# Layer 1 of a two-layer network: up values by seven block products, and layernorms on ScalarE

## The chip, the cores and the metric

The kernel runs on one core of a Trainium2 chip. The metric is the device time of one execution in microseconds (us). TensorE does matrix products into PSUM, VectorE, ScalarE and GpSimd work on elements, and SyncE issues transfers. The page of the profile calls them PE, DVE, ACT, POOL and SP; PEld is TensorE's loading of weights.

## The reference, cut to what matters

Two layers work on x of shape (4, 512, 256). Each normalises the rows and adds an attention branch and a feed-forward branch. Layer 0 (an mLSTM with its own MLP, and a low-rank mixture of experts) is the same in both kernels. Layer 1 is the place of the change:

```python
def _layernorm(x, axis=-1, eps=1e-05):
    m = jnp.mean(x, axis=axis, keepdims=True)
    v = jnp.var(x, axis=axis, keepdims=True)
    return (x - m) / jnp.sqrt(v + eps)
...
def _L1_ffn_ref(x, w_gate, w_up, w_down):
    h = jax.nn.silu(jnp.einsum('bsh,hi->bsi', x, w_gate)) * jnp.einsum('bsh,hi->bsi', x, w_up)
    h_sparse = _sparsify_2to4(h)      # of each four neighbours the two largest by |h| stay
    return jnp.einsum('bsi,ih->bsh', h_sparse, w_down)
...
xn = _layernorm(x, axis=-1)
x = x + _L1_attn_ref(xn, L1_attn_weight_qkv, L1_attn_weight_out) + _L1_ffn_ref(xn, L1_ffn_w_gate, L1_ffn_w_up, L1_ffn_w_down)
```

`w_gate` and `w_up` are 256 x 1024, `w_down` is 1024 x 256, all in float32. The attention of layer 1 is among the 4 entries of the first axis, 16 heads of 16, causal.

## The kernel before

The 512 rows are cut into NJ = 4 blocks j of 128 rows. A block holds its rows of all four batch entries, so a transposed block `xT` (tile `xnT`) is two tiles (k = 0, 1) of 128 features by S = 512 columns.

**Order.** Nothing is ordered by hand. Generators (`flow`) yield the time at which they can go on, and the class `Clock` keeps a model of each engine's time (`took`, `issue`), by which the generators are interleaved while the program is written. Each engine then executes its instructions strictly in that order. All instructions pass through one helper, so the profile gives line 222 for nearly all of them, and work is told apart by tile names.

**A block of layer 1.**
- `front_rows(j)` makes the layernorm (`layernorm`: bn_stats, bn_aggr, a power of -1/2 on GpSimd, a scaling, on VectorE) into tile `xn`, and eight transposes `pt` with two ScalarE copies into `xnT`. `following_rows(j + 1)` runs it beside block j and then `other_sides`, four subtractions of quarters of `xnT` into tile `xd`. Block 0's layernorm runs at the end of layer 0.
- `rows(j)` takes the 1024 columns of the feed-forward in two halves, f0 = 0 and 4. A half is 512 columns, or four chunks of 128, in the tile `hs`.
- The gate values of a half come from seven block products in place of eight (`Sevens.pairs`). The weights' sides (`sides`: four GpSimd operations for each pair of chunks) are made once, ahead, in rooms of tiles that layer 0 has left. Each product is two matmuls of 128x128 by 128x256. They go into the PSUM tiles `x`, `y` and the standing bank `z`, in a chain: products x and y, ScalarE copies of x to z and of y to a room (`copied`), further products added in the same banks, a ScalarE copy of x, and VectorE additions (`added`) of PSUM to the copies. The rooms lie in the tiles `w_up` and `w_down` of layer 0. The chain's second part, `last`, runs as a generator of its own.
- `gate` applies ScalarE's Silu into `hs`.
- The up values of a half are four chunks `up` of 128x512 from `project` (two matmuls each, weights in tile `lora`), each multiplied into `hs` by VectorE.
- `sparsified` makes ScalarE's absolute values `hm`, comparisons `c`, `rest`, `t`, `keep`, and two multiplications on VectorE.
- `attention_rows` makes q, k and v (`qk_ps`, `v_ps`, copied by ScalarE); `attend_rows` the attention, with products `pd` on GpSimd and their sums `sc`, `o` on VectorE, then transposes `pt<-ident,o`.
- `finish_rows` sums the output `yp` of a block over 10 terms, adds it to x and writes it out. It runs late, beside the next blocks.

A matmul of the program is two instructions in the profile. Tiles reused from layer 0 keep that layer's name: `w_gate` is here the down weights, `wguT` the gate weights, `WdT` the qkv weights.

Of the kernel before, what the change touches and what calls it, by code (L numbers as in the profile page):

```python
# [9 lines left out]
AF = mybir.ActivationFunctionType  # L10
ALU = mybir.AluOpType
AX = mybir.AxisListType

P = 128
B, S, D = 4, 512, 256
NJ = S // P
KD = D // P
H, DQK, DV = 8, 16, 32
FF, NF = 1024, 1024 // P
# [15 lines left out]
def layers_kernel(ctx: ExitStack, tc: tile.TileContext, io: dict, out: bass.AP):  # L35
# [17 lines left out]
    class Clock:  # L53
# [100 lines left out]
        def issue(self, kind, op, args, kw, us=None, what=None):  # L154
            operands = [*args, *kw.values()]
            aps = [o for o in operands if hasattr(o, "tensor") and hasattr(o, "offset")]
            out, ins = aps[0], aps[1:]
            if "out" in kw:
                out = kw["out"]
                ins = [i for i in aps if i is not out]  # L160

            shared = [i for i in ins if str(i.space) == "PSUM"]
            start = max(self.free[kind], self.ready(out, *shared, reads=True, but=kind),
                        self.ready(*ins, but=kind))
            if kind == "pe" and start > self.free["pe"]:
                self.stalls.append((self.free["pe"], start - self.free["pe"], out.tensor.name))
            if kind == "act":
                f = next((o for o in operands if isinstance(o, AF)), None)
                if f is not None and f not in self.ANY:
                    table = f in self.SILU  # L170
                    if table != self.table:
                        start += 1.28
                    self.table = table
            if us is None:
                us = self.took(kind, op, out, ins, operands, start)
            end = self.free[kind] = start + us
            end += 0.2 if kind == "pe" else 0.08
            for ap, w, r in [(out, end, 0.0), *((i, 0.0, end) for i in ins)]:
                lo, hi = self.part(ap)
                name = ap.tensor.name  # L180
                spans = self.known(name)
                if w and lo == 0 and len(spans) > 64:
                    spans[:] = [s for s in spans if s[2] > start - 50 or s[3] > start - 50]
                spans.append((lo, hi, w, r, kind))
# [12 lines left out]
    def new(pool, shape, tag, bufs=None, dtype=F32):  # L197
        count[0] += 1
        kw = {} if bufs is None else {"bufs": bufs}
        t = pool.tile(shape, dtype, tag=tag, name=f"{tag}_{count[0]}", **kw)  # L200
        clock.ring(t, (id(pool), tag), bufs or (2 if tag in ("xn", "xnT") else 1))
        return t
# [244 lines left out]
    def inv_sqrt(o, i):  # L447
        n = i.shape[1]
        pool.tensor_tensor(out=o, in0=i, in1=mhalf[:, 0:n], op=ALU.pow)

    def layernorm(pool, x, xn, ms=None):


        stats = new(pool, [P, B, 6], "stats", 2)
        mv = new(pool, [P, B, 2], "mv", 2)
        rstd = new(pool, [P, B], "rstd", 2)
        for b in range(B):
            dve.bn_stats(stats[:, b, :], x[:, b, :])
            dve.bn_aggr(mv[:, b, :], stats[:, b, :])
            yield flow.spare()  # L460
        var = mv[:, :, 1]
        dve.tensor_scalar(rstd, var, 1e-5, None, ALU.add)
        if ms is not None:
            dve.reciprocal(ms, rstd)
        inv_sqrt(rstd, rstd)
        if ms is not None:

            dve.tensor_tensor(ms, ms, var, ALU.mult)
            dve.tensor_scalar(ms, ms, 1e-6, None, ALU.add)
        yield from flow.wait(rstd)  # L470
        for b in range(B):
            dve.tensor_scalar(
                xn[:, b, :], x[:, b, :], mv[:, b, 0:1], rstd[:, b : b + 1], ALU.subtract, ALU.mult
            )
# [26 lines left out]
    def sides(w, rooms, by):  # L501

        v = w.rearrange("p k (q m c) -> p k q m c", m=2, c=P)
        for i in range(len(rooms) // 3):
            q = slice(2 * i, 2 * i + 2)
            a11, a12, a21, a22 = v[:, 0, q, 0, :], v[:, 1, q, 0, :], v[:, 0, q, 1, :], v[:, 1, q, 1, :]
            s1, s2, s4 = rooms[3 * i : 3 * i + 3]
            for o, a, b, op in ((s1, a21, a22, ALU.add), (s2, s1, a11, ALU.subtract),  # L510
                                (a21, a11, a21, ALU.subtract), (s4, a12, s2, ALU.subtract)):
                by.tensor_tensor(out=o, in0=a, in1=b, op=op)

        def kept(n):
            return lambda q: rooms[q // 2 * 3 + n][:, q % 2, :]

        return {"a11": lambda q: v[:, 0, q, 0, :], "a12": lambda q: v[:, 1, q, 0, :],
                "a22": lambda q: v[:, 1, q, 1, :], "s3": lambda q: v[:, 0, q, 1, :],
                "s1": kept(0), "s2": kept(1), "s4": kept(2)}
# [93 lines left out]
    both = ctx.enter_context(tc.tile_pool(name="both", bufs=2))  # L613
    xTs = {}

    def front_rows(j):

        xn = new(both, [P, B, D], "xn")
        yield from layernorm(both, x_sb[j], xn)
        xT = new(both, [P, KD, S], "xnT")  # L620
        for k in range(KD):
            yield from flow.wait(xn, banks=1)
            transposed(lambda l, k: xn[:, l, k * P : (k + 1) * P], xT, k)
        yield from flow.wait(xT)
        xTs[j] = xT
# [891 lines left out]
    f_down = weight("f_down", D, "w_gate")  # L1517
    aoT = weight("aoT", D, "w_out")
    rooms = [t[:, KD * FF + i * 2 * P : KD * FF + (i + 1) * 2 * P] for i in range(3)]
    for name, n in (("wvg", KD * V), ("w_og", KD * D)):  # L1520
        t = new(wts, [P, n], name)
        rooms += [t[:, i : i + 2 * P] for i in range(0, n - 2 * P + 1, 2 * P)]
    rooms = [t.rearrange("p (q c) -> p q c", c=P) for t in rooms]
    gate_sides = sides(f_gate, rooms[0:6], pool)
    t = [new(wts, [P, NF * D], name) for name in ("w_up", "w_down")]
    copies = [t[i % 2][:, i // 2 * S : (i // 2 + 1) * S] for i in range(8)]

    def room():
        copies.append(copies.pop(0))
# [4 lines left out]
    with ExitStack() as l1:  # L1534
# [165 lines left out]
        def room_of_sides():  # L1700
            return new(wk1, [P, 4, HALF], "xd", 2)

        def following_rows(j):
            yield from front_rows(j)
            bs[j] = other_sides(xTs[j], room_of_sides(), dve)

        def rows(j):
            if j + 1 < NJ:
                flow.add(following_rows(j + 1), 3, turn=-2)
            b = bs[j]  # L1710
            while j >= 2 and j - 2 not in out_of:
                yield flow.soon(0.2)
            for f0 in range(0, NF, 4):
                hs = new(wk1, [P, 4, S], "hs", 4)
                gated.setdefault(j, []).append(hs)
                there, done = set(), set()

                def part(m, half, hs=hs):
                    return hs.rearrange("p (i m) n -> p i m n", m=2)[
                        :, :, m, half * HALF : (half + 1) * HALF]  # L1720

                def gate(m, half, t, free, part=part, there=there):
                    act.activation(part(m, half), t.rearrange("p (i n) -> p i n", i=2), AF.Silu)
                    there.add((m, half))
                    free()

                def then(hs=hs, done=done, n=2 * j + f0 // 4):
                    while len(done) < 4 or sum(map(len, halves.values())) < n:
                        yield flow.soon()
                    yield from sparsified(j, hs)  # L1730

                first, last = sevens.pairs(gate_sides, b, f0 // 2, gate)
                yield from first
                flow.add(last, turn=-2)
                for n in range(4):
                    yield from flow.wait(banks=1)
                    up = mm_ps("up")
                    project(up, f_up, xTs[j], (f0 + n) * P, P)
                    clock.held.add(up.tensor.name)

                    def rest(n=n, up=up, hs=hs, there=there, done=done):
                        while (n % 2, 0) not in there or (n % 2, 1) not in there:
                            yield flow.soon(0.2)
                        yield from flow.wait(up, hs[:, n, :])
                        clock.held.discard(up.tensor.name)
                        dve.tensor_tensor(hs[:, n, :], up, hs[:, n, :], ALU.mult)
                        done.add(n)

                    flow.add(rest(), turn=-2)
                flow.add(then(), turn=-1)  # L1750
            flow.add(finish_rows(j), turn=1)
# [52 lines left out]
```

## Time and profile before

| | |
|---|---|
| median of 3 runs | 759.52 us (759.51 to 759.94) |
| the profiled execution | 760.13 us, its span 758.4 us |
| busy in the span: PE, PEld | 751.7 and 539.0 us |
| DVE, ACT, POOL | 490.0, 234.9 and 163.4 us |
| DMA | 25.44 MB, mean 34 GB/s |

The times of the runs are of whole executions. The profile is of one execution of its own: its span goes from the first to the last instruction, and 1.73 us lie around it. The busy times overlap; how they lie in the two layers is told with the prediction.

### The profile page before, as it was taken

To read this page: it belongs to the slowest core of one execution; us is meant where nothing else is said; L and a number is where in the kernel's file an instruction comes from. 1 tells how busy PE (TensorE), PEld (TensorE's weight loads), DVE (VectorE), ACT (ScalarE), POOL (GpSimd) and SP (SyncE) were. 2 spreads that over 40 slices of the span, in tenths; PEclk is the share of its full clock that TensorE was granted. 3 is DMA by queue.
4 is the path that set the end of the run, shared out by engine and by line. 5 is a ranking of instruction groups with operands and counts; after the bars stand their busy time and mean duration, and the time that the engine had idled before them with its cause. 6 is when DMAs were issued, how large, how long until landed. Compare 5 with 4: busy or idle time off the path is not lost.

```text
span 758.4 us, 9984 instructions
## 1 busy us (share of the span) xinstructions
PE 751.7 (99%) x3890; PEld 539.0 (71%) x3890; DVE 490.0 (65%) x1099; ACT 234.9 (31%) x479; POOL 163.4 (22%) x154
## 2 busy tenths in 40 slices
PE   9999999999999999999999999999999999999998
PEld 6786878766578776766778775756766668668587
DVE  5777586766644887654377745433678989788571
ACT  3334133432222333131323122120253642542310
POOL 6230052150132050113020023210322333112000
PEclk9999999999999999999999999999999999999999
DMA  7930000030000020000030310001000000000001
GB/s 232 301 112 1 2 0 1 6 108 0 2 1 1 30 83 1 1 1 1 1 111 1 111 44 14 1 0 56 0 1 0 1 1 25 4 0 29 0 15 42
DMA packets 18959, 25.44 MB, mean 34 GB/s; under 512 B 2784, under 2 KB 12768, under 8 KB 18912
## 3 DMA queue, kind: packets, MB, share of 16 engines
q1 hardware_dynamic: 17824, 24.53, 10.2%
q8 instruction: 30, 0.49, 0.3%
q10 hardware_dynamic: 1088, 0.28, 0.2%
q14 instruction: 17, 0.14, 0.1%
HBM read 22.65 MB, written 2.16 MB: 33 GB/s over the span
## 4 chain that ended last, share of the span: by engine, by line
PE 91%; DVE 7%; ACT 1%; issue 0%; POOL 0%; DVEq 0%; POOLq 0%
PE chunk L222 18%; PE yp L222 16%; PE up L222 15%; PE acc L222 11%; PE gp L222 7%; PE x L222 3%; PE qk_ps L222 3%; PE pt L222 2%; PE vp L222 2%; PE o_ps L222 2%; PE lp L222 2%; PE v_ps L222 2%; PE y L222 2%; PE qk L222 1%; PE sums L222 1%; PE hv L222 1%
## 5 line engine op out<-in xcount | busy, mean ns | idle before, releaser
L222 ACT ACTIVATE sl<-chunk 128x256 f32<-128x256 f32 x132 | 50.6, 384 | 122.2 <-PE chunk L222 106.6
L222 PE MATMUL chunk<-low,lora 128*128 128x256 f32 (+1 forms) x384 | 85.8, 383 | 1.6 <-DVE he_pair L222 1.1
L222 PE MATMUL chunk<-xnT,wguT 128*128 128x256 f32 (+1 forms) x384 | 83.2, 383 | 0.0
L222 PEld LDWEIGHTS chunk<-xnT,wguT 128*128 128x128 f32 (+1 forms) x384 | 64.2, 181 | 20.4 <-issue 8.8
L222 PEld LDWEIGHTS chunk<-low,lora 128*128 128x128 f32 (+1 forms) x384 | 63.7, 181 | 17.1 <-issue 5.1
L222 DVE SCALAR_TENSOR_TENSOR sl<-sl,chunk 128x256 f32<-128x256 f32 x132 | 54.7, 414 | 30.0 <-ACT sl L222 29.4
L222 PE MATMUL gp<-featT,w_gate 128*128 128x512 f32 x128 | 60.3, 593 | 0.0
L222 PE MATMUL up<-featT,w_up 128*128 128x512 f32 x128 | 60.3, 593 | 0.0
L222 PE MATMUL up<-xnT,lora 128*128 128x512 f32 x128 | 58.4, 592 | 0.0
L222 PE MATMUL yp<-w_down,hid 128*128 128x256 f32 x256 | 56.6, 379 | 0.0
L222 PE MATMUL yp<-w_gate,hs 128*128 128x256 f32 x256 | 56.1, 379 | 0.0
L222 PEld LDWEIGHTS yp<-w_down,hid 128*128 128x128 f32 x256 | 48.4, 190 | 8.2 <-issue 1.9
L222 PEld LDWEIGHTS yp<-w_gate,hs 128*128 128x128 f32 x256 | 48.6, 190 | 6.6
L222 DVE SCALAR_TENSOR_TENSOR tmp<-tmp,gp 128x512 f32<-128x512 f32 x32 | 22.0, 687 | 43.1 <-ACT tmp L222 43.1
L222 ACT ACTIVATE tmp<-gp 128x512 f32<-128x512 f32 x32 | 19.1, 598 | 91.3 <-PE gp L222 91.3
L222 POOL TENSOR_TENSOR ss<-ss,mhalf 128x32 f32<-128x32 f32 x4 | 22.0, 5503 | 101.2 <-DVE ss L222 101.2
L222 PEld LDWEIGHTS up<-featT,w_up 128*128 128x128 f32 x128 | 24.1, 190 | 27.6 <-issue 26.5
L222 PEld LDWEIGHTS gp<-featT,w_gate 128*128 128x128 f32 x128 | 24.0, 190 | 27.5 <-issue 26.8
L222 PE MATMUL acc<-WdT,hid 128*128 128x256 f32 (+1 forms) x192 | 41.1, 382 | 0.0
L222 PE MATMUL acc<-tmp,lora 128*128 128x512 f32 x80 | 40.4, 595 | 0.0
L222 PEld LDWEIGHTS up<-xnT,lora 128*128 128x128 f32 x128 | 24.3, 190 | 22.5 <-issue 21.0
L222 POOL TENSOR_TENSOR pd<-k,q 128x512 f32<-128x512 f32 (+2 forms) x12 | 23.3, 1944 | 70.7 <-ACT k L222 44.1
(252 smaller groups left out, 1263.8 us busy)
## 6 DMA issues: line engine op xcount, KB each, us to landing
ct<-m_dram SPq DMA_DIRECT2D x8, 1024.0 KB, 8.1
x<-in_x SPq DMA_DIRECT2D x3, 512.0 KB, 9.7
out<-x SPq DMA_DIRECT2D x6, 256.0 KB, 2.1
w_gate<-in_w_gate SPq DMA_DIRECT2D x1, 1024.0 KB, 6.7
w_up<-in_w_up SPq DMA_DIRECT2D x1, 1024.0 KB, 7.7
w_down<-in_w_down SPq DMA_DIRECT2D x1, 1024.0 KB, 10.2
wguT<-in_f_gate SPq DMA_DIRECT2D x1, 1024.0 KB, 4.8
lora<-in_f_up SPq DMA_DIRECT2D x1, 1024.0 KB, 4.9
```

Of the source, the lines that this page charges most:

```text
L222: return tc.keep_in_program_order(f(*args, **kw))
```

## The change

Three things change in layer 1.
- The up values of each block's second half (f0 = 4) come from `sevens.pairs` with the up weights' sides. The four `project` chunks of that half go. `up_too` multiplies each of the four quarters of a half by the gate in `hs`, as soon as the gate's quarter is there.
- The up weights' sides are made by four more GpSimd operations ahead, in rooms 6 to 8, which take in the tiles `wq` and `wk` of layer 0. One of the eight rooms for copies becomes a place for squares that nobody reads, so seven are left.
- The layernorms of blocks 1 to 3 are made by `norm_by_scalar`: four ScalarE sums (`accum_out`), four shifts, four squares with sums, four scalings, with two small VectorE operations and GpSimd's power between. The generator starts at once, not 3 us later.

The writer's model also learns that an instruction with `accum_out` writes two things.

```diff
+            extra = kw.get("accum_out")
...
+            ins = [i for i in ins if i is not extra]
...
-            for ap, w, r in [(out, end, 0.0), *((i, 0.0, end) for i in ins)]:
+            written = [out] if extra is None else [out, extra]
+            for ap, w, r in [*((o, end, 0.0) for o in written), *((i, 0.0, end) for i in ins)]:
...
-    def front_rows(j):
+    def front_rows(j, norm=None):
...
-        yield from layernorm(both, x_sb[j], xn)
+        yield from norm(x_sb[j], xn) if norm else layernorm(both, x_sb[j], xn)
...
-    for name, n in (("wvg", KD * V), ("w_og", KD * D)):
+    for name, n in (("wvg", KD * V), ("w_og", KD * D), ("wq", KD * P), ("wk", KD * P)):
...
-    gate_sides = sides(f_gate, rooms[0:6], pool)
+    gate_sides, up_sides = (sides(w, room, pool) for w, room in (
+        (f_gate, rooms[0:6]), (f_up[:, :, FF // 2 :], rooms[6:9])))
...
+    unread_squares = copies.pop()[:, 0:D]
...
+        def norm_by_scalar(x, xn):
+
+            sums = new(sm, [P, 3, B], "sums", 2)
+            mean, ss, rstd = (sums[:, n, :] for n in range(3))
+            for b in range(B):
+                act.activation(xn[:, b, :], x[:, b, :], AF.Identity, accum_out=mean[:, b : b + 1])
+                yield flow.soon(0.5)
+            yield from flow.wait(mean)
+            dve.tensor_scalar(mean, mean, -1.0 / D, None, ALU.mult)
+            yield from flow.wait(mean)
+            for b in range(B):
+                act.activation(xn[:, b, :], x[:, b, :], AF.Identity, bias=mean[:, b : b + 1])
+                yield flow.soon(0.5)
+                act.activation(
+                    unread_squares, xn[:, b, :], AF.Square, accum_out=ss[:, b : b + 1])
+                yield flow.soon(0.5)
+            yield from flow.wait(ss)
+            dve.tensor_scalar(ss, ss, 1.0 / D, 1e-5, ALU.mult, ALU.add)
+            inv_sqrt(rstd, ss)
+            yield from flow.wait(rstd)
+            for b in range(B):
+                act.mul(xn[:, b, :], xn[:, b, :], rstd[:, b : b + 1])
+                yield flow.soon(0.5)
...
-            yield from front_rows(j)
+            yield from front_rows(j, norm_by_scalar)
...
-                flow.add(following_rows(j + 1), 3, turn=-2)
+                flow.add(following_rows(j + 1), 0, turn=-2)
...
-                for n in range(4):
+
+                def up_too(m, half, t, free, part=part, there=there, done=done):
+                    def rest():
+                        h = part(m, half)
+                        while (m, half) not in there:
+                            yield flow.soon(0.2)
+                        yield from flow.wait(h, t)
+                        dve.tensor_tensor(
+                            h, t.rearrange("p (i n) -> p i n", i=2), h, ALU.mult)
+                        done.add((m, half))
+                        free()
+
+                    flow.add(rest(), turn=-2)
+
+                if f0:
+                    first, last = sevens.pairs(up_sides, b, 0, up_too)
+                    yield from first
+                    flow.add(last, turn=-2)
+                for n in range(0 if f0 else 4):
```

## The prediction

> **What bounds the kernel now.** I read the page first, then the busy time by stage, TensorE's timeline in the second layer, the groups of instructions by shape, and the timelines of VectorE and GpSimd where they meet.
>
> ```profile
> PE 751.7 (99%) x3890; PEld 539.0 (71%) x3890; DVE 490.0 (65%) x1099; ACT 234.9 (31%) x479; POOL 163.4 (22%) x154
> ...
> PEclk9999999999999999999999999999999999999999
> ...
> PE 91%; DVE 7%; ACT 1%; issue 0%; POOL 0%; DVEq 0%; POOLq 0%
> ```
>
> TensorE is busy all the time at the full granted clock, and 91% of the chain of waits is its own work. The stage that the change touches begins with the matmul that opens layer 1's PSUM bank z, at 536.87 us. The stage view gives (columns: time, then busy time and instructions of PE, PEld, DVE, ACT, POOL):
>
> ```profile
> 0.00:536.87 536.87, 533.43 (x3032) 381.51 (x3033) 322.66 (x845) 153.97 (x334) 116.63 (x123) 1.00 0.14 43
> 536.87:758.40 221.53, 218.28 (x859) 157.45 (x857) 167.38 (x254) 80.90 (x145) 46.77 (x31) 1.00 0.03 10
> ```
>
> In layer 1 TensorE works 218.28 of 221.53 us, and the rest is almost all the end, after its last matmul. VectorE has 167.38, ScalarE 80.90. So what counts is how much matmul time goes, and how much of it comes back as waits of TensorE, which takes its instructions strictly in the order written. TensorE's timeline shows the prices (start, length, instructions):
>
> ```profile
> 642.52 1.03 PE L222 MATMUL z<-xnT,wguT 128*128 128x256 f32 x4
> 643.38 1.03 PE L222 MATMUL y<-xnT,wguT 128*128 128x256 f32 x4
> 644.25 1.37 PE L222 MATMUL pt<-ident,o 128*128 128x128 f32 x8
> 645.45 1.03 PE L222 MATMUL x<-xd,wguT 128*128 128x256 f32 x4
> 646.32 3.60 PE L222 MATMUL up<-xnT,lora 128*128 128x512 f32 x8
> 649.75 1.03 PE L222 MATMUL x<-xd,wguT 128*128 128x256 f32 x4
> ```
>
> From start to start a block product takes 0.865 us (644.25 - 643.38 and its neighbours), and two chunks of up values 649.75 - 646.32 = 3.43, so 1.715 each. The transposes of o at 644.25 take 1.37 instead of the usual 1.04: a wait of 0.34 for VectorE, the longest that TensorE has in this layer before its last matmul.
>
> **The block products.** In each of the four blocks four chunks of up values, 4 x 1.715 = 6.86 us, become seven products, 7 x 0.865 = 6.05. That is 0.81 a block and 3.24 us over four. All of it is on the path, since TensorE is. The order of the changed kernel's instructions has exactly this exchange on TensorE; layer 0 is in the same order as before.
>
> The products need 3 more ScalarE copies a block and 2 more VectorE additions. Rows (line, operation, out<-in, shapes, count | busy, mean ns):
>
> ```profile
> L222 ACT COPY z<-x 128x512 f32<-128x512 f32 x8 | 4.6, 570 | 19.9 <-PE x L222 19.9
> L222 ACT ACTIVATE xn<-xn,r 128x256 f32<-128x256 f32 x16 | 6.8, 498 | 8.9 <-POOL r L222 8.9
> L222 ACT COPY o<-v 128x256 f32<-128x256 f32 x4 | 1.6, 400 | 0.0
> L222 ACT ACTIVATE fu<-fa 128x32 f32<-128x32 f32 x4 | 0.9, 229 | 0.1
> ```
> ```profile
> L222 DVE TENSOR_SCALAR xn<-x,mv,rstd 128x256 f32<-128x256 f32 x12 | 7.3, 669 | 1.1 <-POOL rstd L222 1.1
> L222 DVE TENSOR_TENSOR w_up<-x,w_up 128x512 f32<-128x512 f32 x8 | 5.5, 682 | 0.0
> L222 DVE BATCH_NORM_STATS2 stats<-x 128x6 f32<-128x256 f32 x12 | 4.9, 405 | 0.0
> L222 DVE BATCH_NORM_AGGREGATE mv<-stats 128x2 f32<-128x6 f32 x12 | 2.2, 182 | 0.4
> L222 DVE TENSOR_SCALAR rstd<-mv 128x4 f32<-128x4 f32 x3 | 1.2, 386 | 0.0
> ```
>
> Copies: about 3 x 0.57 = 1.7 us of ScalarE a block, 6.9 in all. Additions: 2 x 0.68 = 1.4 of VectorE, 5.5 in all. The four multiplications by the gate keep their number and size; two now read SBUF alone. Taken at nothing, because TensorE does other work beside them; the cover is the attention products and up chunks that the order sets between the steps of a chain. Without it each copy is worth its 0.57 on the path. GpSimd's four preparations of the up weights, at 0.73 each (the gate's own took that) 2.9 us, stand behind the gate's eight, which end at 495.7. The up weights were issued at 427.5 and GpSimd then idles 45.9 us, so they cost nothing; uncovered they would cost 2.9.
>
> **The layernorms.** VectorE loses per block 4 x 0.405 + 4 x 0.182 + 0.386 + 4 x 0.669 = 5.4 us, 16.3 over three. It gains two tiny scalings (0.16 each, 1.0 in all). With the additions its 167.4 becomes about 158. No gain for TensorE follows, as its only long wait for VectorE is the 0.34 above.
>
> ScalarE gains 16 instructions a block: four sums and four squares at 0.40 (o<-v, both sides in SBUF) and four shifts and four scalings at 0.50 (xn<-xn,r, a scale per partition), 7.2 us, less about 0.1 of overlap for each in a row. Eight of them also write a sum, which no instruction before does. Call that extra e. Its bounds: nothing, if the sum comes with the pass; and, far up, one more 512-wide copy, 0.57, with more not excluded. The nearest row is the smallest kind of separate instruction, 128x32 at 0.229, which overlaps its neighbour; I take e = 0.2. ScalarE then goes from 80.90 to 80.9 + 6.9 + 3 x (7.2 + 1.6) = about 114 of 221 us. On average that is no bound. The table loads stay eight in number.
>
> [...]
>
> In ScalarE's queue the new instructions stand ahead of copies that TensorE waits for. I followed the order with the row times for the two narrow places.
> - Block 0: squares of block 1's rows stand before the copy of x into z at about 548.3 us. TensorE has only one product, 0.865, to do meanwhile and waits 0.06 for this copy today. The copy slips by some 0.2 at e = 0, plus e for the square in front, plus a second e for the sum before.
> - Block 1: from its second block product to the first of its second gate half TensorE has 9 x 0.865 + 5 x 1.715 = 16.4 us of work. In that stretch ScalarE has about 12.5 us, with two table loads of 1.28 and 4 us in which nothing is ready for it: no more than 1 us to spare against 7 sums, 7e.
>
> Together this is about 9e - 1 us: nothing at e = 0.1, 0.8 at e = 0.2, 3.5 at e = 0.5. The transposes of block 2's rows come some 0.2 us after the last scaling can end, and those of block 3's rows 6 us after, so block 3 costs nothing. Today's 0.34 at o moves to another block (GpSimd's last product for block 1 ends some 3 us before o is wanted, VectorE has an addition and 1.92 to do) and I leave it as it is. At the end nothing new is late: VectorE is done with the last half about 7 us before TensorE wants it, as today (741.0 against 748.2).
>
> **Sum.** The profiled execution took 760.13 (span 758.4 and 1.73 around it), 0.61 over the median 759.52. 760.13 - 3.24 + 0.8 = 757.7 on its scale, and 757.1 on the median's.
>
> **Rivals.**
> - *ScalarE's queue becomes what TensorE waits for* (ends slower). Place: the two stretches above. Price: 9e - 1. It eats the gain at e = 0.47 and is slower beyond 0.2% from e = 0.64; at e = 0.8 the time is 759.52 - 3.24 + 6.2 = 762.5. For it: no row has a summing ScalarE instruction, and the normalised rows now go through ScalarE, VectorE, ScalarE, VectorE, GpSimd and ScalarE again, each behind other work. Against it: ScalarE idles half the layer, and no ScalarE instruction of 128x64 or less takes over 0.26. [...] Chance 0.17.
> - *VectorE and GpSimd collide more.* VectorE instructions that read only SBUF stretch while GpSimd multiplies (a line of GpSimd's timeline and one of VectorE's: two comparisons that take 1.28 undisturbed, as at 606.21, take 3.44):
>
> ```profile
> 624.19 2.61 POOL L222 TENSOR_TENSOR pd<-k,q 128x1024 f32<-128x1024 f32 x1
> ```
> ```profile
> 623.91 3.44 DVE L222 TENSOR_TENSOR rest<-hm 128x512 bf16<-128x512 f32 x2
> ```
>
>   The change adds two such multiplications a block and takes away four scalings a block in three blocks. Block 0's two fall beside block 1's q and k products. If they and the following ones each pass 2.2 us on, once, to ScalarE's absolute values and so to TensorE, the time is 757.1 + 2.2 = 759.3, no change that can be told. For it: that row; against it: TensorE has 5 to 16 us of other work there. Chance 0.17, with all smaller mixtures that end near no change.
> - *The change does not do what it says.* Excluded for the matmuls by the order; the sums are in it too.
>
> **The numbers.** A measurement of this kernel can tell about 0.2%, 1.5 us, from no change. The forecast's case, waits up to 1.7 us more than today, has 0.66, all of it faster than 758.0. The range goes from 756.0 (e = 0 and a part of today's small waits gone: 759.52 - 3.24 - 0.3) to 760.6, which takes in the collision and e up to 0.58; above it lies most of the slower rival's 0.17, below it 0.03.
>
> **What would show it.** In the profile after: up<-xnT,lora with 64 instructions in place of 128 and 112 new ones of 128x256 on x, y and z; VectorE near 158 us and ScalarE near 114 in layer 1; summing instructions near 0.6 us. TensorE's waits for ScalarE, in blocks 0 and 1, near 0.8 us in all. Wrong if the summing ones pass 0.9, if TensorE stands over 1.7 us longer than today before x, z or pt, or if a wait for GpSimd's multiplications ends last.

## The result, and the profile after

The changed kernel takes 756.37 us (median of 5 runs, 756.18 to 756.64) against 759.70 (759.51 to 760.06) for the kernel before in the same rounds: a ratio of 0.9956, with a 95% interval of 0.9943 to 0.9969, or 3.3 us less.

The page of the profile after, its lines on busy time, granted clock and chain (the helper that issues all instructions now stands on line 225, and on line 226 in two of the later runs):

```profile
span 754.9 us, 10142 instructions
...
PE 748.1 (99%) x3938; PEld 548.4 (73%) x3938; DVE 480.0 (64%) x1074; ACT 259.1 (34%) x563; POOL 171.9 (23%) x158
...
PEclk9999999999999999999999999999999999999999
...
PE 92%; DVE 6%; POOL 1%; ACT 1%; issue 0%; POOLq 0%; DVEq 0%
```

TensorE bounds the kernel as before, now with 3.6 us less work. The stage view, cut at the matmul that opens z, places all of it in layer 1 (columns as in the prediction):

```profile
0.00:536.87 536.87, 533.43 (x3033) 381.67 (x3034) 322.88 (x845) 154.16 (x336) 119.67 (x128) 1.00 0.13 43
536.87:754.90 218.03, 214.72 (x907) 166.76 (x905) 157.16 (x229) 104.96 (x227) 52.23 (x30) 1.00 0.03 10
```

The first stage is what it was. In the second TensorE's work falls from 218.28 to 214.72, VectorE's by 10 us, and ScalarE's rises by 24. From the matmul that opens z to the start of the last group of output products the layer takes 201.00 us (536.81 to 737.81); before, it took 204.42 (536.87 to 741.29). Below, "the layer's work" means this stretch. The exchange of matmuls (groups by shape: count | busy, mean ns | idle before):

```profile
L225 PE MATMUL up<-xnT,lora 128*128 128x512 f32 x64 | 29.3, 592 | 0.0
L225 PE MATMUL x<-xd,lora 128*128 128x256 f32 x32 | 8.2, 379 | 0.0
...
L225 PE MATMUL x<-xd,wq 128*128 128x256 f32 x16 | 4.1, 379 | 0.0
```

64 up matmuls in place of 128, and the new products in groups of 16 and 32. In the whole layer TensorE's list of waits has one line before its last matmul:

```profile
PE pt L225 <- DVE o L225: 0.2, 1, 0.2
```

So 3.24 of the 3.42 us are the products at the prediction's prices. The other 0.18 is not traced. It is not idle time: TensorE idles 0.12 us in this stretch before and 0.19 after.

The ScalarE groups show the layernorms' price:

```profile
L225 ACT ACTIVATE xn<-xn,sums 128x256 f32<-128x256 f32 x12 | 5.5, 498 | 0.0
L225 ACT ACTIVATE w_down<-xn 128x256 f32<-128x256 f32 x12 | 5.1, 427 | 0.0
L225 ACT ACTIVATE xn<-x 128x256 f32<-128x256 f32 x12 | 5.1, 423 | 0.0
L225 ACT ACTIVATION_READ_ACCUMULATOR w_down<-xn 128x1 f32 x12 | 2.4, 204 | 0.0
L225 ACT ACTIVATION_READ_ACCUMULATOR xn<-x 128x1 f32 x12 | 2.4, 199 | 0.0
```

A summing instruction is two: the pass, and a read of the accumulator of 0.20 us. What the read adds is seen where instructions stand in a row, on ScalarE's timeline (start, length):

```profile
582.39 0.42 ACT L225 ACTIVATE xn<-x 128x256 f32<-128x256 f32 x1
582.71 0.19 ACT L225 ACTIVATION_READ_ACCUMULATOR xn<-x 128x1 f32 x1
582.80 0.36 ACT L225 COPY v<-v_ps 128x256 f32<-128x256 f32 x1
```

The next copy starts 0.09 us after the read does. The extra that the prediction called e is 0.09, not 0.2.

### The profile page after: what moved, and what is told of

Its sections match the earlier page's. It is cut to its first block, busy times and chain, and to the rows that moved or that the text cites. A ratio compares the mean times of both kernels' runs of the same rounds, so it can differ in the third digit from the quotient of the medians.

```text
span 754.9 us, 10142 instructions
## 1 busy us (share of the span) xinstructions
PE 748.1 (99%) x3938; PEld 548.4 (73%) x3938; DVE 480.0 (64%) x1074; ACT 259.1 (34%) x563; POOL 171.9 (23%) x158
## 4 chain that ended last, share of the span: by engine, by line
PE 92%; DVE 6%; POOL 1%; ACT 1%; issue 0%; POOLq 0%; DVEq 0%
PE chunk L225 18%; PE yp L225 16%; PE acc L225 11%; PE up L225 11%; PE gp L225 7%; PE x L225 5%; PE y L225 3%; PE qk_ps L225 3%; PE pt L225 2%; PE vp L225 2%; PE o_ps L225 2%; PE lp L225 2%; PE v_ps L225 1%; PE z L225 1%; PE qk L225 1%; PE sums L225 1%
## 5 line engine op out<-in xcount | busy, mean ns | idle before, releaser
L225 POOL TENSOR_TENSOR pd<-k,q 128x512 f32<-128x512 f32 (+2 forms) x12 | 27.5, 2298 | 99.3 <-ACT k L225 78.4
L225 PEld LDWEIGHTS acc<-WdT,hid 128*128 128x128 f32 (+1 forms) x192 | 32.9, 189 | 7.5 <-issue 3.2
L225 DVE TENSOR_TENSOR tmp<-chunk,sl 128x256 f32<-128x256 f32 x80 | 34.0, 425 | 2.8
```

What stands on the lines that cost most here:

```text
L225: return tc.keep_in_program_order(f(*args, **kw))
```

## The experiments

The question is whether the two parts are independent, as the prediction's sum took them (products gain, layernorms cost a little), or whether one needs the other. A third theory came up on the way: that only the written order, the place of a few instructions, decides. Each ratio is to the kernel before, run again in the same rounds; its median was then between 759.73 and 759.80. "The writer" is the part of the program that interleaves the generators by its model of the engines' times.

**The products alone**: blocks 1 to 3 are normalised by VectorE as before the change.

```diff
-            yield from front_rows(j, norm_by_scalar)
+            yield from front_rows(j)
-                flow.add(following_rows(j + 1), 0, turn=-2)
+                flow.add(following_rows(j + 1), 3, turn=-2)
```

> The up values of the second half from seven products, but the layernorms of blocks 1 to 3 by VectorE as in the kernel before. Theory A (TensorE's instruction time sets the time; the layernorms' place is free either way): the products' 3.24 us go, 756.4 us, with at most 0.5 us of new waits. Theory B (VectorE, full from 617 to 645 us in the kernel before, could not have carried two more additions a block, and moving the layernorms away is what lets the products pay): 1.5 us or more come back, 758 us or more, and TensorE's waits for VectorE grow by as much.

Measured: 761.35 us (759.64 to 761.82), ratio 1.0014 (1.0005 to 1.0023), as theory B expected. TensorE does 3.24 us less and the kernel is no faster. TensorE's timeline has the reason (the profiled execution is one of 761.82):

```profile
585.51 1.13 PE L225 MATMUL x<-xd,lora 128*128 128x256 f32 x4 [0.95 <-DVE w_up L225]
...
644.30 0.77 PE L225 MATMUL pt<-ident,o 128*128 128x128 f32 x5 [2.05 <-DVE o L225]
644.91 1.47 PE L225 MATMUL z<-xnT,wguT 128*128 128x256 f32 x4
646.17 1.91 PE L225 MATMUL qk_ps<-WdT,xnT 128*128 128x256 f32 x4
647.87 1.48 PE L225 MATMUL v_ps<-WdT,xnT 128*128 128x256 f32 x4
```

0.95 and 2.05 us of waiting for VectorE. After the second wait the same groups of four matmuls take 1.47 to 1.91 us in place of 1.03, and the granted clock from 640 to 650 us is 0.83 (1.00 in the changed kernel). VectorE is nearly full there (columns: time, then busy PE, PEld, DVE, ACT, POOL, and the granted clock):

```profile
617.00:645.00 28.00, 25.95 (x125) 21.85 (x124) 27.32 (x43) 7.00 (x15) 10.91 (x7) 1.00 0.06 19
```

27.32 of 28 us, against 26.24 in the kernel before and 25.93 in the changed kernel. A share of 25.93 goes with hardly a wait (0.19 us), so the share alone does not tell when TensorE begins to wait. Shorter stretches show the clock behind the long wait:

```profile
645.00:649.00 4.00, 4.00 (x13) 3.17 (x12) 1.51 (x2) 3.28 (x5) 0.00 (x0) 0.57 0.00 0
645.50:648.50 3.00, 3.00 (x9) 2.34 (x8) 1.01 (x1) 2.28 (x4) 0.00 (x0) 0.50 0.00 0
```

Four us at 0.57 are an estimated 1.7 us of work lost. The 11 runs have two levels: four at a mean granted clock of 1.000 took 759.64 to 760.12, seven at 0.998 took 761.34 to 761.82. So the waits eat the gain to nothing, and where the clock falls after the long one, 1.7 us more are lost.

**The layernorms alone**: second halves by whole chunks again, no sides of the up weights.

```diff
-                if f0:
+                if False:
...
-                for n in range(0 if f0 else 4):
+                for n in range(4):
```

> The layernorms of blocks 1 to 3 by ScalarE, but all up values from whole chunks as in the kernel before. Theory A: no change that can be told, 759.3 to 760.2 us; ScalarE gains about 18 us of busy time, VectorE loses about 15, TensorE loses at most its 0.34 us wait for o. Theory B: some of the 3.3 us come from the layernorms alone, 758.5 us or less.

Measured: 767.16 us, ratio 1.0096 (1.0081 to 1.0112). Neither theory expected a loss.

```profile
613.44 0.33 PE L225 MATMUL pt<-ident,o 128*128 128x128 f32 x1 [0.64 <-DVE o L225]
617.08 1.33 PE L225 MATMUL pt<-ident,o 128*128 128x128 f32 x5 [3.31 <-DVE o L225]
```

The transposes of o wait 0.64 and 3.31 us for VectorE, though VectorE has less work in the layer (156.19 us) than before the change (167.38). The granted clock from 610 to 620 is 0.84. All waits for VectorE in the layer are 4.9 us, and its work takes 211.14 us, 6.7 more than before.

**More ScalarE work**: the change, with one more square behind each sum and each square (24 instructions of 0.42 that nobody reads), put past the writer's model, so that all else keeps its order.

```diff
+        def untold(x):
+            tc.keep_in_program_order(nc.scalar.activation(unread_squares, x, AF.Square))
...
+                untold(x[:, b, :])
```

> The changed kernel with one more ScalarE square of 128x256, whose result nobody reads, behind each of the 24 summing instructions, unknown to the writer's model, so that all other instructions keep their order. Each costs about 0.31 us start to start, so the price e of a sum rises from the 0.1 us seen to 0.41. The prediction's working (9e - 1 us of TensorE's waits) expects 2.7 us more than the changed kernel: 759.1 us. Theory A with the slack read from the trace after (0.31 us before the copy into z in block 0, where ScalarE has no idle time from 546.5 us on; 1.24 us against 1.03 idle in block 1; nothing in the others) expects 0.5 to 0.8 us more: 756.9 to 757.2 us.

Measured: 757.21 us, ratio 0.9966 (0.9953 to 0.9978), 0.84 more than the change. TensorE's longest wait in the layer is for the copy of x into z in block 1, in the second gate half, the later of the two places that the prediction named:

```profile
598.75 1.13 PE L225 MATMUL x<-xd,wvg 128*128 128x256 f32 x4 [0.48 <-ACT z L225]
```

From start to start this product comes 0.64 us later behind its neighbour than in the change (1.51 against 0.87), and in block 0 the one at 548.90 comes 0.35 later (1.22 against 0.87).

The extra per summing instruction rose by some 0.3 (0.33 from the start of such a square, at 547.90, to the start of the copy behind it), to about 0.4 us. By the prediction's 9e - 1 that costs 2.7; it cost 0.84. The places were right and the slope three times too steep. Of the seven sums and squares that it counted in block 1, three end before ScalarE stands idle for 1.02 us at 584.53, so only four reach the copy; of the two in block 0, one ends before 0.41 us of idle time.

**First halves by products too**, in all blocks (rooms for the sides in three more tiles of layer 0).

```diff
-        (f_gate, rooms[0:6]), (f_up[:, :, FF // 2 :], rooms[6:9])))
+        (f_gate, rooms[0:6]), (f_up, rooms[6:12])))
...
-                if f0:
-                    first, last = sevens.pairs(up_sides, b, 0, up_too)
+                first, last = sevens.pairs(up_sides, b, f0 // 2, up_too)
```

> The changed kernel with the up values of the first halves from seven products too, the further sides in rooms of the tiles AgT, AuT and BdT of layer 0. Theory A: another 3.24 us go, less some 0.1 us for each chain that has no other work beside it, 753.2 to 753.9 us. Rival: ScalarE (105 us in layer 1, then about 112) or VectorE (157, then about 163) ends last in blocks 0 and 3, where few other products lie between the steps of a chain, and gives back 1.5 us or more: 754.6 us or above.

Measured: 760.69 us, ratio 1.0005 (0.9996 to 1.0013), again in two levels: 759.06 to 759.25 at a clock of 1.000, 760.58 to 760.88 at 0.997 to 0.998. By the prediction's price TensorE has another 3.24 us less to do, and the kernel is slower than the change. The rival gave the amount, but for blocks 0 and 3; the long waits all stand in block 1:

```profile
596.97 1.13 PE L225 MATMUL x<-xd,lora 128*128 128x256 f32 x4 [1.23 <-ACT w_up L225]
601.79 1.13 PE L225 MATMUL x<-xd,lora 128*128 128x256 f32 x4 [2.83 <-DVE w_down L225]
```

VectorE works 9.93 of the 10 us from 590 to 600, and just as much in the changed kernel, where TensorE does not wait. What differs is that no up chunks are left to stand between the steps of two chains; that this is the reason is not shown by a run of its own.

**Is it only the place of o?** The two parts alone again, with the transposes of o written 3 us later.

```diff
+            yield clock.ready(o) + 3.0
```

> The kernel with the products only (layernorms by VectorE), and the transposes of o written 3 us later than the writer's model finds o ready. Theory A2 (TensorE's own time decides; what the products alone lost are waits at a transpose that the writer, blind to how long VectorE stands beside GpSimd's products, put too early): the 2.05 us wait and the slower clock behind it go, 756.4 to 757.9 us (the 0.95 us wait for an addition may stay). Theory B2 (VectorE has no room for the layernorms and the new additions together, wherever the transposes stand): the lateness comes up at the next place, 759 us or more.

> The kernel with ScalarE's layernorms only, and the transposes of o written 3 us later in the same way. VectorE has 11 us less to do here than in the kernel before, so A2 expects the 0.64 + 3.31 + 0.77 us of waits for o and the slowed clock to go and the time of the kernel before to come back: 759.3 to 760.8 us. If moving the layernorms itself costs (their chain through three engines being late for the transposes of xn), 763 us or more stays.

Products alone: 761.31 us, ratio 1.0021 (1.0012 to 1.0030), at a clock of 0.999 or 1.000 in all runs. The wait for o is gone and others have come:

```profile
587.69 1.09 PE L225 MATMUL pt<-ident,xn 128*128 128x128 f32 x6 [1.32 <-DVE xn L225]
612.47 1.13 PE L225 MATMUL x<-xd,lora 128*128 128x256 f32 x4 [0.75 <-DVE w_down L225]
623.52 1.09 PE L225 MATMUL pt<-ident,xn 128*128 128x128 f32 x6 [1.10 <-DVE xn L225]
```

Two of the three are for xn, which the changed kernel's VectorE no longer makes. So B2 held. Layernorms alone: 761.93 us, ratio 1.0028 (1.0018 to 1.0039), 5.2 less than in the first order and between the two expectations. There the order accounts for most of the loss, but not all: waits of 0.88, 0.32 and 0.60 us elsewhere remain. The theory that only the place of o decides falls for the products and holds in part for the layernorms.

**The parts alone with another model**: from layer 1 on the writer's model holds VectorE for up to 2 us where it meets GpSimd, since with the products alone a VectorE subtraction of 0.41 us took 1.97 beside a GpSimd product of 1.98 (at 637.68).

```diff
+            self.hold = 0.0
...
-                us += max(0.0, min(us, self.free["pool"] - start))
+                us += max(0.0, min(max(us, self.hold), self.free["pool"] - start))
...
+        clock.hold = 2.0
```

> The products only (layernorms by VectorE), with the writer's model told, from layer 1 on, that GpSimd may hold a VectorE instruction that reads SBUF alone for up to 2 us. Layer 0 is in its old order. A2 (the waits are the writer's, not VectorE's): a better told order finds other work for TensorE, 756.4 to 757.6 us. B2 (VectorE has no room for the layernorms beside the new additions in blocks 0 to 2): a third order loses too, 759 us or more, with TensorE waiting for VectorE for 2 us or more.

> ScalarE's layernorms only, with the writer's model told the same. A2: 759.2 to 760.5 us, as the kernel before. 761.5 us or more if the layernorms on ScalarE cost something where whole chunks of up values leave TensorE more work.

Products alone: 758.90 us, ratio 0.9990 (0.9981 to 0.9999), between the two expectations. The best of three orders gains 0.9 of the 3.24 us. The waits for VectorE are shorter, two in the same places and one new (0.63 for w_up, 1.21 for o, 0.32 for w_up), and VectorE is as full from 617 to 645, 27.32 of 28 us. Layernorms alone: 763.56 us, ratio 1.0050 (1.0037 to 1.0063), a loss as in the second expectation, still waiting for o:

```profile
615.91 0.77 PE L226 MATMUL pt<-ident,o 128*128 128x128 f32 x5 [2.71 <-DVE o L226]
```

Followed back in this trace, o waits for GpSimd's products of v (606.99 to 612.38), these for the exponentials at 603.58, and at the head of that chain GpSimd stood at the next block's layernorm, before its power, until 592.12. The products of k and q behind it began at 593.68, though ScalarE had copied q and k for the first two of them by 580.7 and 585.0 (the bracket holds the whole idle time, 32.81 us):

```profile
592.12 1.38 POOL L226 TENSOR_TENSOR sums<-sums,mhalf 128x4 f32<-128x4 f32 x1 [32.81 <-DVE sums L226]
...
593.68 3.52 POOL L226 TENSOR_TENSOR pd<-k,q 128x512 f32<-128x512 f32 x2
```

By this a layernorm that takes longer from its first to its last step holds the attention up through GpSimd's queue. The third product could not have begun earlier, as its k was copied by 593.57, so the queue cost at most the time of the first two (all three took 5.83 us). The layernorms alone in their first order show the same, with the power at 592.36 after 32.82 us. The reading was not tested by a run of its own.

**The change with the layernorms started 3 us later**, as before the change. It is also the products alone with one thing more, the layernorms on ScalarE.

```diff
-                flow.add(following_rows(j + 1), 0, turn=-2)
+                flow.add(following_rows(j + 1), 3, turn=-2)
```

> The changed kernel with the layernorms' generator starting 3 us later, as the kernel before has it. If the start does not matter: 756.2 to 757.2 us. If the early start is what gets the rows through ScalarE in time, TensorE waits for xn by up to 3 us in blocks 0 and 1: 757.5 to 762 us.

Measured: 757.72 us, ratio 0.9973 (0.9963 to 0.9983). The time is in the second range, but its reason is not in the trace: TensorE's waits there are 0.49 for o and 0.32 and 0.18 for two steps of chains, none for xn. The stretch in which VectorE was nearly full with the products alone is now:

```profile
617.00:645.00 28.00, 28.00 (x129) 23.08 (x128) 21.17 (x30) 17.91 (x45) 15.60 (x8) 1.00 0.06 20
```

VectorE works 21.17 us in place of 27.32, and TensorE does not stop. This makes a ladder of single steps at full clock: before 759.8; products 759.7 (the four runs); layernorms to ScalarE 757.7; started at once 756.4. Each step also changes the written order: against the best order of the products alone (758.9), the layernorms' step is 1.2 us.

**The hold in the whole program**: the changed kernel, with a model that holds VectorE for up to 2 us, in layer 0 too.

```diff
-                us += max(0.0, min(us, self.free["pool"] - start))
+                us += max(0.0, min(2.0, self.free["pool"] - start))
```

> The changed kernel, with one number of the writer's model changed: a VectorE instruction that reads SBUF alone may be held by GpSimd for up to 2 us, not only for its own length again. The written order changes, the work does not. A2: the changed kernel has only about 0.5 us of TensorE's waits left in layer 1, so at best 756.0 us; 756.0 to 757.0. If the order of the changed kernel was luck, a wait of 1 us or more comes in somewhere: 757.5 us or more.

Measured: 762.46 us, ratio 1.0033 (1.0020 to 1.0046). In the profiled execution (761.08, the fastest of five) the loss is in layer 0, whose order changed too: TensorE waits 3.9 us for GpSimd's tmp at 103.82, the granted clock from 100 to 200 us is 0.98, and layer 1 begins 4.1 us later. Layer 1's own work, in another order than the changed kernel's, takes 201.32 us, 0.3 more. So the changed kernel's layer 1 does not hang on one lucky order. The products alone under nearly the same model took 203.70 us for that work, so in this order too the layernorms on ScalarE, started at once, are worth 2.4.

**First halves by products, except in block 1**, where the waits of the fourth run stood.

```diff
-                if f0:
-                    first, last = sevens.pairs(up_sides, b, 0, up_too)
+                if f0 or j != 1:
+                    first, last = sevens.pairs(up_sides, b, f0 // 2, up_too)
...
-                for n in range(0 if f0 else 4):
+                for n in range(0 if f0 or j != 1 else 4):
```

> The changed kernel with the up values of the first halves from seven products in blocks 0, 2 and 3, not in block 1, where the version with all four waited 4.5 of its 5 us. A2: 756.4 less 3 x 0.81 us, plus 0.3 us for each chain that has no other work beside it, 754.0 to 755.0 us, the fastest of all. If VectorE or ScalarE is too late in other blocks too, 756 us or more.

> The version with the first halves' up values from seven products in blocks 0, 2 and 3, made whole: the one side that overwrote the weights which block 1 reads in whole chunks has a room of its own (half of the room for unread squares). The run before it did the same matmuls, with block 1 reading overwritten weights. 754.4 to 755.2 us by the account that each half costs TensorE 0.81 us less if no wait comes in; 756 us or more if the new room, free only when layer 0 ends, makes a chain late.

In the first of the two, block 1's whole chunks read up weights that one of the sides has replaced in part, so block 1 is computed from other weights; the second puts that side in a room of its own. They take 754.63 and 754.67 us, both as expected; the second's ratio is 0.9933 (0.9921 to 0.9946), 1.7 us less than the change. By the prediction's prices three more exchanges are 3 x 0.81 = 2.4 us. TensorE's idle time in the layer's work is 0.63 us, 0.44 more than in the change, and the rest of the difference is not traced. Waits of 0.31 for z in block 0 and 0.19 for o stand out:

```profile
555.13 1.10 PE L225 MATMUL x<-xd,wq 128*128 128x256 f32 x4 [0.31 <-ACT z L225]
...
638.05 0.77 PE L225 MATMUL pt<-ident,o 128*128 128x128 f32 x5 [0.19 <-DVE o L225]
```

The second version is faster than both kernels.

## Why the prediction was right, and where it was not

- **The products, 3.24 us off TensorE's path: right**, in count and price. The layer's work fell by 3.42, and the median by 3.33.
- **The new waits, 0.8 us: mis-sized.** They did not come, and this is nearly all of the difference between the fall that was forecast, 2.4 us, and the 3.3 measured. The term was 9e - 1 at e = 0.2. Measured, e is 0.09, at which the formula gives about nothing. The formula was wrong too. It let the 1 us to spare in block 1 pay for a wait in block 0, though the two are apart: at e = 0.09 block 0 alone would have cost 0.4. And its slope was too steep, as the run with more squares showed (0.84 for 2.7). The guess of e from the smallest separate instruction was right in its length (0.20 against 0.229) but not in how much of it lies beside its neighbours.
- **The additions and copies of the chains at nothing: right for this kernel, but not for the reason given.** The reason was that TensorE does other work beside them. The products alone have that work too, and TensorE waits 0.95 and 2.05 us for VectorE there. The zero held because the layernorms had left VectorE, which the sum did not use; so far it was luck.
- **ScalarE near 114 us in the layer: 104.96.** The instructions are as long as said (0.42 and 0.50, with 0.20 for the read), but they overlap: the layernorms alone add 99.08 - 80.90 = 18.2 us of busy time to ScalarE, 6.1 a block, where I had 8.8. The 8.8 took e too large and left out the 0.1 of overlap for each instruction that the prediction itself named.
- **VectorE near 158: 157.16.** The wait for o did not move to another block, as I had it: it stands in block 2 before and after (GpSimd's third round of products of v ends at 640.68 and 636.61), and it did not shrink. From start to start the transposes take 639.24 - 637.96 = 1.28 us, 0.41 over the usual 0.865, where it was 645.45 - 644.25 = 1.20 before, 0.34 over. The 0.19 in the list of waits is only the longest gap among them:

```profile
637.96 0.49 PE L225 MATMUL pt<-ident,o 128*128 128x128 f32 x3
638.64 0.77 PE L225 MATMUL pt<-ident,o 128*128 128x128 f32 x5 [0.19 <-DVE o L225]
639.24 1.03 PE L225 MATMUL x<-xnT,wguT 128*128 128x256 f32 x4
```

- **Block 0's copy into z slipping by 0.2 + 2e: it did not.** In the changed kernel it starts at 548.20, 0.04 after the matmuls that it copies end; before, it was 0.03.
- **"No gain for TensorE follows" from the layernorms' move: wrong.** I judged it by the waits of the kernel before, where VectorE makes TensorE wait only 0.34 us. The products add 6.0 us to VectorE (173.37 us in the layer with the products alone, 167.38 before), and with those TensorE waits 3.0 us, as much as the products gain. The sum treated the parts as independent. In the three orders tried the products alone gave +1.6, +1.6 and -0.9 us and the layernorms alone +7.4, +2.2 and +3.8, so alone the one gains 0.9 at best and the other loses, and together they gain all of it. With the layernorm's start held at 3 us, its move to ScalarE is worth 2.0 us on top of the products (1.2 against their best order).
- **The rival of ScalarE's queue** is answered by the run with more squares: even with e near 0.4 the kernel is 2.6 us faster than before. ScalarE is the slower engine for these layernorms (6.1 us a block, against 5.4 by VectorE's rows of before), but the fuller engine was VectorE (27.32 of 28 us with the products alone), and moving them off it made the kernel faster (759.7 to 757.7 at full clock).
- **The rival of VectorE** did not decide the changed kernel. VectorE is what TensorE waits for with the products alone; whether by collisions with GpSimd, as the rival had it, or by the plain amount of its work, no run separates.

What stays open is how much of the layernorms' loss when alone is the written order and how much the longer chain. Three orders gave 2.2 to 7.4 us, and the hand-over through GpSimd was read from two traces and not tested.

## What to carry to other kernels

When TensorE is the bound and work is taken off it, look for the engine that gets the replacement's extra steps: if that one is nearly full for a long stretch (here 27.3 of 28 us), the gain can come back as waits, and moving other work off it is then part of the same change. Judge the parts of a change together as well as alone, because a wait that the profile of before doesn't show can be made by one part and removed by the other. Where each step shortens the bound engine by a fixed amount, apply it block by block and leave out the blocks where the waits appear.

## What the runs showed of the hardware

- After some of TensorE's waits of 2 to 4 us the granted clock fell, and after others it did not; what decides it no run shows. Behind the wait of 2.05 us it was 0.50 from 645.5 to 648.5 in the profiled execution of the products alone (0.57 from 645 to 649, 0.83 from 640 to 650), and the runs of that kernel at a mean of 0.998 are 1.7 us longer than those at 1.000, with nothing between. It was 0.84 from 610 to 620 with the wait of 3.31 us in the layernorms alone, and 0.98 from 100 to 200 with the wait of 3.9 us in the run with the hold in the whole program. A wait of 2.83 (first halves too, profiled at 759.25 us) and one of 2.71 (layernorms alone, other model) left the clock at 1.00.
- A VectorE instruction that reads and writes SBUF alone took far longer beside a GpSimd product than without one. In the products alone with the other model, a subtraction of 0.41 us took 1.97 beside a product of 1.98:

```profile
637.09 1.97 DVE L226 TENSOR_TENSOR xd<-xnT,xd 128x256 f32<-128x256 f32 x1
639.32 0.41 DVE L226 TENSOR_TENSOR xd<-xnT,xd 128x256 f32<-128x256 f32 x1
```
```profile
636.80 1.98 POOL L226 TENSOR_TENSOR pd<-v,sc 128x1024 f32<-128x1024 f32 x1 [1.37 <-DVE o L226]
```
